# Four layers in one kernel: how the second layer's last image is scaled and the third layer begins, and the order of the last layer's first convolution

## The chip, the cores and the metric

The kernel runs on one core of a Trainium2 chip. The metric is the device time of one execution in microseconds (us); three runs of the kernel before gave 6766.48 (median), 6764.02 and 6773.46. A profiled execution leaves the times of every instruction on the engines: TensorE (PE, with its weight loads PEld), VectorE (DVE), ScalarE (ACT), GpSimd (POOL), and SyncE (SP), which issues all the DMA transfers here.

## The reference

An input of 4 images, 192 channels, 56 x 56 pixels, float32, goes through four layers one after the other. All shapes stay `(4, 192, 56, 56)`.

```python
# layer 0: local attention; batch statistics first
mean = jnp.mean(x, axis=(0, 2, 3)); var = jnp.var(x, axis=(0, 2, 3))
qkv = conv1x1(bn(x), qkv_w, qkv_b)            # 6 heads of 32
attn = softmax(conv7x7(cat(q * scale, k), dm_w) + dm_b + rel_bias, axis=2)   # 49 weights a pixel
out = sum over the 49 neighbours of attn * v
x1 = x + conv1x1(out, proj_w); x = x1 + conv1x1(gelu(conv1x1(x1, c1_w)), c2_w)

# layer 1: a gate for each image and channel
g = relu(bn(conv1x1(x, wg1))).mean((2, 3)) ... filt      # filter from image 0
y = sum(pool7x7(x) * filt); y = relu(bn(y @ w1d[:, :, 1].T + b1d))
x = x * y[:, :, None, None] + x

# layer 2: windows of 8 x 8 at a step of 6, attention in each, folded together;
#          a depthwise 3x3 gate; then gelu, depthwise 3x3, product, projection
# layer 3:
xc, z = split(conv1x1(layer_norm(x), in_proj_w))
xc = silu(depthwise3x3(xc, conv_w) + conv_b)
... four selective scans over xc: rows and columns, forward and backward ...
out = x + conv1x1(layer_norm(y) * silu(z), out_proj_w)
```

The code has three parts: `layers01` for the first two layers, `layer2`, `layer3`. What the code calls the gate (`sc`) is `1 + y` of layer 1.

## The kernel before

**An order written out by a planner.** The instructions of PE, DVE, ACT and POOL are issued in an order that the class `Order` works out when the kernel is built. Every piece of work is a Python generator, a thread, with a place (a number: a smaller one is more urgent). It yields the engine, an assumed duration and the buffers that it needs (`on_pe`, `on_dve`, `on_act`, `on_pool`, `on_sp`), and then issues its instructions. `run` picks again and again the thread with the smallest planned start plus 0.05 us for each unit of its place. It may also yield a condition, such as a mark that another thread sets or the count of a layer's open threads (`order.open`). The assumed durations decide the order alone; on the chip each engine works through its list in that order, and semaphores see to it that data are there and memory is free. The DMA queue of SP is not in the planner's hands: the tile framework orders it.

**Layers 0 and 1** (L370 to L1097). First each image is loaded whole (L402: the first into `x`, the other three into two buffers `xs`), and `bn_stats` goes over it in 14 pieces of 448 pixels (L405). Behind these loads SP issues those of the weights (L406) and of zeros for the padding in `vmem`. The statistics make `bn_c`, which PE needs for its first matmuls (L440). Attention follows: PE makes logits, DVE sums over the neighbours into `oa` and `ob` (L807 to L825), and `mlp` reads these by transposes (L854), and stores each chunk to `mid` in DRAM (L943). When an image is done, `gate(b)` works out `sc` (L1063 to L1066); then, for each of 7 chunks, it loads both halves of the channels from `mid` into an `xc` buffer (L1072), multiplies each half by `sc` (ACT, L1077, for images 0 to 2; POOL, L1080, for image 3) and stores the result (L1082). Those stores are layer 2's input, image by image.

**Layer 2** (L1105 to L1731) starts its preparation when the attention sums are done: weights, small constants, cleared buffers. At L1214 it waits until no thread of layers 0 and 1 is open, then gives their memory back and takes its own. From there: clears of `xns` (DVE, L1228), `qs`, `ks` and `accs` (POOL, L1231, L1234). Then bands of 12 rows go through `front` (loads of `bxl` L1293, edges on POOL L1298 to L1307, layer norm L1249 to L1271, projections L1318), `quad` (attention in four windows: copies on POOL L1607, PE L1617 and L1637, DVE L1650 to L1661, ACT, PE, DVE L1711), `back`, and in chunks of 8 rows through `head`, `grow` (buffer `z1`) and `tail`. The depthwise convolutions of `head` and `tail` are `dwconv` (L1397, L1399): nine taps, and within a tap 2 or 3 independent parts.

**Layer 3** (L1734 to L2244) begins with seven chunks of 8 rows of image 0 in `begin(0, c)`: edges of `pad` on POOL (L1866 to L1872), layer norm (L1825 on DVE, square on ACT, L1838 on PE, two ACT operations, L1844 on DVE), projections L1878 on PE into `pad` by ACT (L1889), then a depthwise 3 x 3 convolution. For image 0 this is done on DVE (L1912 for the first tap, L1914 for eight more, each adding to what the last one left in `u`), for half the channels at a time; after each half the thread yields to PE and ACT for that half of `z` (L1935, L1939). For images 1 to 3 PE does the convolution with diagonal matrices (L1921). `begin(b, c + 1)` may start when chunk c's `pad` is written, and its place is 6 behind that of c. Scans follow (`scan`, L2116 on: DVE L2128, L2144, L2160, POOL L2167, PE L2138, L2183); the first row scans run while later chunks are begun, and the columns (L1975) need all seven.

**Memory.** Tiles come from stacks on the left and on the right of SBUF. `const`, `per` and `p1` of layers 0 and 1 lie on the left, from the bottom up in the order in which they were opened, with `oa` and `ob` in `per`. Layer 2's `xns`, `qs`, `ks`, `accs` are laid out from the bottom of the left after these are closed, in this order. What reuses memory waits for the last reader and writer of the old tiles at that address, stores to DRAM among them.

Of the kernel before, what the change touches and what calls it, by code (L numbers as in the profile page):

```python
# [227 lines left out]
def pixels(ap):  # L228

    return ap.rearrange("(h p) n -> p h n", p=HALF)  # L230
# [122 lines left out]
def on_act(*n, takes=(), table=None, ready=None):  # L353
    return "ACT", sum(0.2 + 0.0009 * i for i in n), takes, table, ready
# [15 lines left out]
def layers01(tc, pools, x_in, packs, aps, dst):  # L370
# [5 lines left out]
    nc = tc.nc  # L376

    ctx, early, dram, banks = pools["01"], pools["01 sums"], pools["dram"], pools["banks"]
    const = ctx.enter_context(tc.tile_pool(name="a_const", bufs=1))
    att = early.enter_context(tc.tile_pool(name="a_att", bufs=1, side="right"))  # L380
    dram = dram.enter_context(tc.tile_pool(name="a_dram", bufs=1, space=DRAM))
# [13 lines left out]
    nc.vector.memset(zero, 0.0)  # L395
    bn_a = const.tile([HALF, 2], F32, name="bn_a")
    bn_c = const.tile([HALF, 2], F32, name="bn_c")
    with tc.tile_pool(name="a_stat", bufs=2) as sp:
        stats = sp.tile([HALF, 2, B * NCHUNK, nc.vector.BN_STATS_DIM], F32, name="stats", bufs=1)
        for b in range(B):  # L400
            t = x[:HALF] if b == 0 else sp.tile([HALF, 2, HW], F32, name="xs")
            nc.sync.dma_start(t, pixels(x_in[b]))  # L402
            for h in range(2):
                for c in range(NCHUNK):
                    nc.vector.bn_stats(stats[:, h, b * NCHUNK + c, :], t[:, h, c * CH : (c + 1) * CH])  # L405
        w = load_packs(nc, const, packs, aps)  # L406
        nc.sync.dma_start(v_bias, aps["vb"].to_broadcast([112, C]))
        for v in vmem:
            for g in range(NG):
                for y in (0, PADW - 3):  # L410
                    nc.sync.dma_start(v[g][:, y : y + 3].rearrange("x y c -> x (y c)"), zero)
                for y in (0, PADW - 3):
                    nc.sync.dma_start(
                        v[g][y : y + 3].rearrange("x y c -> y x c"), zero.rearrange("p (x c) -> p x c", c=64)
                    )
        mv = sp.tile([HALF, 2, 2], F32, name="mv", bufs=1)
        for h in range(2):
            nc.vector.bn_aggr(mv[:, h, :], stats[:, h].rearrange("p a b -> p (a b)"))
        std = sp.tile([HALF, 2], F32, name="std", bufs=1)
        nc.vector.tensor_scalar_add(std, mv[:, :, 1], EPS)  # L420
        nc.scalar.activation(std, std, AF.Sqrt)
        nc.vector.reciprocal(std, std)
        nc.vector.tensor_mul(bn_a, w["a96.bn_gamma"], std)
        nc.vector.tensor_mul(bn_c, mv[:, :, 0], bn_a)
        nc.vector.tensor_sub(bn_c, w["a96.bn_beta"], bn_c)
# [65 lines left out]
    def keep(name, shape, n, rows=128, pool=per):  # L491
        return [pool.tile([rows, *shape], F32, name=f"{name}{i}") for i in range(n)]
# [10 lines left out]
    for t in (*qk_in, *xc, *lg):  # L503
# [11 lines left out]
        rsum=keep_att("rsum", [2, 28], 3, 112),  # L515
        qs=qk_sum,
        lg=lg,
        oa=keep("oa", [28, 128], 2, 112),
        ob=keep("ob", [28, 64], 2, 112),
        hm=keep("hm", [CH], 2),  # L520
    )
    take, done = order.take, order.done
# [509 lines left out]
    def gate(b):  # L1032

        yv = p1.tile([HALF, 2], F32, name="yv")
        for h in range(2):
            yield on_dve(H * DCT, 49, 49)
            r2 = p1.tile([HALF, DCT * DCT], F32, name="pool_y")
            nc.vector.tensor_reduce(
                r2.rearrange("p (a b) -> p a b", b=DCT),
                pool_of[b][:, h].rearrange("p (a i b) -> p a b i", i=H // DCT, b=DCT),  # L1040
                AX.X,
                ALU.add,
            )
            nc.vector.tensor_mul(r2, r2, filt[:, h])
            nc.vector.tensor_reduce(yv[:, h : h + 1], r2, AX.X, ALU.add)
        done(pool_of[b])
        yield on_dve(2)
        nc.vector.tensor_scalar_mul(yv, yv, 1.0 / 64.0)
        yield on_pe(4 * 80, "bank")
        pt = take()  # L1050
        py = pt[:HALF, :2]
        for h in range(2):
            for k in range(2):
                nc.tensor.matmul(
                    py[:, h : h + 1],
                    w["a96.w1T"][:, k, HALF * h : HALF * h + HALF],
                    yv[:, k : k + 1],
                    start=(k == 0),
                    stop=(k == 1),
                )  # L1060
        yield on_dve(2, 2, 2)
        sc = p1.tile([HALF, 2], F32, name="sc")
        nc.vector.tensor_mul(sc, py, s1)  # L1063
        done(pt)
        nc.vector.tensor_add(sc, sc, t1)
        nc.vector.tensor_scalar(sc, sc, 0.0, 1.0, ALU.max, ALU.add)  # L1066
        passed.add(("gate", b))
        for c in range(NCHUNK):
            px = slice(c * CH, (c + 1) * CH)
            yield on_sp("xc")  # L1070
            xt = take("xc")
            nc.sync.dma_start(xt[:HALF], pixels(mid[b])[:, :, px])  # L1072

            for h in range(2):
                if b < B - 1:
                    yield on_act(CH, ready=None if h else order.end + 3)
                    nc.scalar.activation(xt[:HALF, h], xt[:HALF, h], AF.Copy, scale=sc[:, h : h + 1])  # L1077
                else:
                    yield on_pool(CH, each=0.0015)
                    nc.gpsimd.tensor_scalar_mul(xt[:HALF, h], xt[:HALF, h], sc[:, h : h + 1])  # L1080
            yield on_sp()
            nc.sync.dma_start(pixels(dst[b])[:, :, px], xt[:HALF])  # L1082
            done(xt)
# [21 lines left out]
def layer2(tc, order, pools, src, packs, aps, dst):  # L1105
# [28 lines left out]
    (p,) = keep("bp", [2, HW], 1)  # L1134
    (apad,) = keep("bapad", [2, 11, W + 2], 1, HALF)
    zpads = keep("bzpad", [3, 12, W + 2], 2)
    z1 = const.tile([128, 3, 10, W], F32, name="bz1")
    g = const.tile([128, 3, 10, W], F32, name="bg")
    pr = p.rearrange("p h (y x) -> p h y x", x=W)
    ident = const.tile([128, 128], F32, name="b_ident")  # L1140
# [70 lines left out]
    nc.vector.tensor_scalar_mul(w["b96.hft_w"], w["b96.hft_w"], 3.0)  # L1211


    yield lambda: order.open["01"] == 0  # L1214
    pools["01"].close()
    p2 = ctx.enter_context(tc.tile_pool(name="b_2", bufs=1, side="right"))
    left = pools["2 quads"].enter_context(tc.tile_pool(name="b_quads", bufs=1))

    def keep_left(name, shape, n, rows=128):
# [3 lines left out]
    qs = keep_left("bq", [2, BR, PADW], 2, HALF)  # L1223
    ks = keep_left("bk", [2, BR, PADW], 2, HALF)
    accs = keep_left("bacc", [2, 2, BR, PADW], 2)
    for i in range(2):
        yield on_dve(1700)
        nc.vector.memset(xns[i], 0.0)  # L1228
        for t in (qs[i], ks[i]):
            yield on_pool(1600, each=0.0009)  # L1230
            nc.gpsimd.memset(t, 0.0)  # L1231
    for t in accs:
        yield on_pool(3400, each=0.0009)
        nc.gpsimd.memset(t, 0.0)  # L1234
# [46 lines left out]
    def front(j):  # L1281
# [3 lines left out]
        rows = ((3, 6), (9, 5)) if r == 0 else ((2, 9),) if r == NB - 1 else ((2, 6), (8, 6))  # L1285

        yield lambda: at["front"] == j and gone("values", 5 * (j - 1) - 1)
        loads = []
        for i, n in rows:
            y = 12 * r + i - 3  # L1290
# [443 lines left out]
def layer3(tc, order, pools, src, packs, aps, dst):  # L1734
# [80 lines left out]
    def gone(*what):  # L1815
        return what in passed
# [30 lines left out]
    def begin(b, c):  # L1847
# [51 lines left out]
        at = y0 - (8 * c - 1)  # L1899
        px = slice(y0 * W, y1 * W)  # L1900
        zt = None
        for h in range(2):
            pz = pc = uh = None
            if b == 0:

                for t in range(9):
                    yield on_dve(n * W, each=0.0012, ready=order.end - 0.3 if t else None)
                    v = pad[:HALF, h, at + t // 3 : at + t // 3 + n, t % 3 : t % 3 + W]
                    uh = rows2(u[:HALF, h, px])
                    wt = w["c96.conv_w"][:, h, t : t + 1]  # L1910
                    if t == 0:
                        nc.vector.tensor_scalar(uh, v, wt, w["c96.conv_b"][:, h : h + 1], ALU.mult, ALU.add)  # L1912
                    else:
                        nc.vector.scalar_tensor_tensor(uh, v, wt, uh, ALU.mult, ALU.add)  # L1914
            if uh is None:
                yield lambda: gone("diagonals")
            for t in range(9 if uh is None else 0):
                yield on_pe(n * W, *(("bank",) if t == 0 else ()), ready=order.end - 0.5 if t else None)
                if t == 0:
                    pc = take()  # L1920
                nc.tensor.matmul(  # L1921
                    rows2(pc[:HALF, : n * W]),
                    diag[:, h, t],
                    pad[:, h, at + t // 3 : at + t // 3 + n, t % 3 : t % 3 + W],
                    start=(t == 0),
                    stop=(t == 8),
                )
            if uh is None:
                yield on_act(n * W)
                nc.scalar.activation(  # L1930
                    u[:HALF, h, px], pc[:HALF, : n * W], AF.Identity, bias=w["c96.conv_b"][:, h : h + 1]
                )
                done(pc)
            yield on_pe(2 * CH, "bank")
            pz = project(2 + h)  # L1935
            yield on_act(CH, takes=() if h else ("gate",))
            if h == 0:
                zt = take("gate")
            nc.scalar.activation(zt[:, h], pz[:HALF, :CH], AF.Identity, bias=in_b[:, 2 + h : 3 + h])  # L1939
            done(pz)  # L1940
# [342 lines left out]
```

## Time and profile before

| what | us |
|---|---|
| three runs: median (lowest, highest) | 6766.48 (6764.02, 6773.46) |
| the profiled execution: its own time | 6756.62 |
| span from its first to its last instruction | 6754.8 |
| DVE busy, share of the span | 5976.0, 88% |
| PE busy | 5757.1, 85% |
| ACT busy | 2615.2, 39% |
| POOL busy | 1414.7, 21% |
| mean granted clock of TensorE | 0.931 of full |

Stretches of the span, from the view by windows (busy us of each engine):

```profile
2928.00:2960.00 32.00, 2.14 (x4) 0.57 (x2) 0.33 (x3) 0.00 (x0) 19.38 (x14) 0.50 0.41 119
2960.00:2993.00 33.00, 18.25 (x95) 11.03 (x97) 6.04 (x6) 9.80 (x17) 18.34 (x23) 0.73 0.06 16
2993.00:3100.00 107.00, 92.87 (x1516) 60.74 (x1502) 79.77 (x167) 54.23 (x96) 31.44 (x60) 0.97 0.07 19
4857.00:4990.00 133.00, 95.09 (x235) 33.75 (x236) 115.45 (x174) 70.66 (x94) 26.75 (x25) 0.85 0.34 88
```

The columns are the stretch, its length, then busy time and number of instructions of PE, PEld, DVE, ACT and POOL, the granted clock, the DMA engines' share, and GB/s. The first two stretches lie between the last gate of layer 1 and the first full bands of layer 2; the last one holds most of layer 3's first convolution. A busy share says how full an engine was, not that it set the end; for that one reads what ended each wait, which the timeline gives in brackets behind an instruction ("[32.47 <-DMA x<-xc]": the engine had been idle for 32.47 us, until that transfer).

### The profile page before, as it was taken

The page shows a single profiled execution, that of the slowest core. Times are in us where ns is not written, and L with a number is a line of the kernel's source. Part 1 is how long each engine was busy: PE and PEld are TensorE (multiplying, and loading weights), DVE is VectorE, ACT ScalarE, POOL GpSimd, SP SyncE. Part 2 cuts the span into 40 slices and gives each one's busy share as a digit, 9 for nine tenths or more (in the row PEclk, how much of TensorE's full clock was granted, in tenths as well). Part 3 has the DMA queues.
Part 4 walks back from the last instruction along what each step waited for, and adds up shares of the span by engine and source line. Part 5 has one row for each costly group of instructions (what it writes and reads, how often), then busy time and mean ns, then how long its engine had stood idle before and what let it go on. Part 6 is the DMA issues. An engine that isn't in the chain of part 4 may idle for free.

```text
span 6754.8 us, 107251 instructions
## 1 busy us (share of the span) xinstructions
PE 5757.1 (85%) x43558; PEld 2642.5 (39%) x43558; DVE 5976.0 (88%) x7515; ACT 2615.2 (39%) x4049; POOL 1414.7 (21%) x1413
## 2 busy tenths in 40 slices
PE   6999889999999995768888788786689889889776
PEld 3444444444444442335444444453222222222211
DVE  2999999999999999838999899898888887887997
ACT  1121121222222121125555455454366566566544
POOL 0000000000000000132222222221025544545564
PEclk9999889999999997889999899998799999999998
DMA  4222112221222112210000000000045555655654
GB/s 107 59 53 59 36 30 62 52 67 34 54 56 73 30 44 75 62 42 16 18 18 16 18 19 15 18 18 22 23 113 134 150 144 131 161 134 138 171 149 118
DMA packets 252042, 462.65 MB, mean 68 GB/s; under 512 B 30388, under 2 KB 237964, under 8 KB 240412
## 3 DMA queue, kind: packets, MB, share of 16 engines
q1 hardware_dynamic: 251548, 455.80, 26.8%
q8 instruction: 343, 5.62, 0.4%
q14 instruction: 151, 1.24, 0.1%
HBM read 238.58 MB, written 62.96 MB: 45 GB/s over the span
## 4 chain that ended last, share of the span: by engine, by line
DVE 26%; PE 20%; issue 4%; ACT 4%; POOL 1%; DMA 1%; SPq 0%; DVEq 0%; POOLq 0%; ACTq 0%
DVE bg L1399 6%; PE bank L1921 4%; DVE st L2160 3%; DVE bxn L1399 3%; PE bank L1878 2%; DVE bank L2144 2%; PE bank L2138 2%; PE bank L2183 2%; PE bank L1562 1%; PE bank L1265 1%; DVE bacc L1711 1%; PE bank L2011 1%; PE bank L1249 1%; DVE e L1650 1%; PE bank L1488 1%
## 5 line engine op out<-in xcount | busy, mean ns | idle before, releaser
L811 DVE TENSOR_TENSOR pr<-vdx,attn 112x1792 f32<-112x1792 f32 (+4 forms) x720 | 1185.9, 1648 | 19.2
L656 PE MATMUL bank<-qk_in,w_a 64*49 64x392 f32 x9408 | 1157.4, 496 | 0.0
L2167 POOL TENSOR_TENSOR da<-st,bc 128x448 f32<-128x448 f32 x672 | 857.3, 1281 | 844.2 <-DVE st L2160 630.3
L816 DVE TENSOR_TENSOR oa<-oa,pr 112x1792 f32<-112x1792 f32 (+1 forms) x423 | 765.0, 1808 | 0.0
L656 PE MATMUL bank<-qk_in,wd 64*49 64x392 f32 x4032 | 691.3, 494 | 0.0
L2160 DVE TENSOR_TENSOR_SCAN st<-da,st,bank 128x448 f32<-128x448 f32 x576 | 646.8, 1132 | 0.7 <-ACT da L2113 0.7
L656 PEld LDWEIGHTS bank<-qk_in,w_a 64*49 64x49 f32 x9408 | 431.7, 120 | 396.1 <-issue 390.4
L1147 POOL MEMSET bxl<- 128x1008 f32 x3 | 2.7, 938 | 2783.3 <-DVE ob L825 2783.3
L2144 DVE TENSOR_TENSOR bank<-bank,bc 128x448 f32<-128x448 f32 x672 | 382.7, 617 | 114.6 <-PE bank L2138 114.1
L331 ACT ACT_TABLE_LOAD x373 | 478.6, 1283 | 6.7
L2113 ACT ACTIVATE da<-da,a_neg 128x448 f32<-128x448 f32 x672 | 413.8, 658 | 111.7 <-DMA da<-dt 109.6
L1399 DVE SCALAR_TENSOR_TENSOR bg<-bzpad,w_b,bg 128x448 f32<-128x448 f32 (+2 forms) x672 | 423.6, 685 | 0.0
L2183 PE MATMUL bank<-da,w_c 128*32 128x448 f32 x1344 | 355.5, 575 | 72.7 <-POOL da L2167 66.9
L816 DVE TENSOR_TENSOR ob<-ob,pr 112x1792 f32<-112x1792 f32 (+3 forms) x282 | 393.1, 1394 | 0.0
L902 ACT ACTIVATE hm<-bank,w_a 128x448 f32<-128x448 f32 x168 | 106.4, 634 | 637.3 <-PE bank L893 617.8
L2138 PE MATMUL bank<-du,w_c 32*128 32x448 f32 x1344 | 261.6, 626 | 105.0 <-DVE du L2128 62.8
L656 PEld LDWEIGHTS bank<-qk_in,wd 64*49 64x49 f32 x4032 | 247.8, 119 | 256.7 <-issue 254.8
L893 PE MATMUL bank<-xc,w_a 128*128 128x448 f32 x672 | 296.8, 571 | 58.6 <-DVE xc L878 58.6
L608 ACT ACTIVATE qk_in<-bank,qk_bias,qk_scale 64x224 f32<-64x224 f32 (+5 forms) x288 | 146.3, 526 | 445.5 <-PE bank L593 443.2
L1488 PE MATMUL bank<-bxn,w_b 128*128 128x448 f32 (+2 forms) x672 | 291.4, 562 | 22.5 <-DVE bxn L1271 17.1
L908 PE MATMUL bank<-hm,w_a 128*96 128x448 f32 x672 | 288.5, 561 | 20.2 <-ACT hm L902 20.2
L1921 PE MATMUL bank<-pad,diag 128*96 128x448 f32 (+2 forms) x756 | 297.4, 543 | 2.3 <-ACT pad L1889 2.3
(309 smaller groups left out, 9908.4 us busy)
## 6 DMA issues: line engine op xcount, KB each, us to landing
da<-dt SPq DMA_DIRECT2D x672, 224.0 KB
vdx<-vmem SPq DMA_DIRECT2D x168, 476.0 KB
bc<-prod SPq DMA_DIRECT2D x224, 224.0 KB
row<-x SPq DMA_DIRECT2D x56, 336.0 KB
x<-x SPq DMA_DIRECT2D x4, 2352.0 KB
vmem<-vt SPq DMA_DIRECT2D x56, 168.0 KB
xc<-x SPq DMA_DIRECT2D x56, 168.0 KB
mid<-xc SPq DMA_DIRECT2D x56, 168.0 KB
```

The costliest lines, as they stand in the source:

```text
L331: self.nc.scalar.preload_act_table_set(table)
L656: nc.tensor.matmul(py[a][outs[g], : 7 * W].rearrange("p (y x) -> p y x", x=W), wt[halves[a], dx], q[halves[a], r, i0 + m : i0 + m + 7, dx ...
L811: nc.vector.tensor_mul(pr, vv, wt)
L816: nc.vector.tensor_add(og, og, before)
L1399: nc.vector.scalar_tensor_tensor(dst, x, wt[:, t : t + 1], dst, ALU.mult, ALU.add)
L1921: nc.tensor.matmul(rows2(pc[:HALF, : n * W]), diag[:, h, t], pad[:, h, at + t // 3 : at + t // 3 + n, t % 3 : t % 3 + W], start=(t == 0), ...
L2113: nc.scalar.activation(da, da, AF.Exp, scale=a_neg[:, k, g : g + 1])
L2138: nc.tensor.matmul(tiles[j][:, :SCH], w["c96.rep"][r], du[r], start=True, stop=True)
L2144: nc.vector.tensor_mul(tiles[j][:, :SCH], tiles[j][:, :SCH], b_)
L2160: nc.vector.tensor_tensor_scan(sts[j][:, r], da[:, r], tiles[j][:, :SCH][:, r], first, ALU.mult, ALU.add)
L2167: nc.gpsimd.tensor_mul(da, sts[j], c_)
L2183: nc.tensor.matmul(py[32 * j : 32 * j + 32, :SCH], w["c128.sum"], das[j], start=True, stop=True)
```

## The change

- The last image's scaling goes through two new small buffers `xg` (one half of one chunk each, 448 values) and always runs on ACT: 14 loads, 14 operations, 14 stores. `xg` and that image's `sc` live in a pool of their own on the right, which is closed with layer 2's.
- When the last gate is known, a mark is set. Layer 2 takes over the memory of layers 0 and 1 when this mark is there and one of their threads is left open, the one that scales. Its fronts of image 3 wait until that thread is done too.
- `oa` and `ob` get a pool that is opened first on the left; `z1` moves to a pool that is opened later.
- The clears of `xns`, `qs`, `ks` are dealt out anew: the first of each on DVE, the second on POOL.
- The statistics at the start load images 1 to 3 in 21 chunks of 448 pixels through five buffers, and both halves of a chunk follow each other.
- In `begin(0, c)` each tap of the convolution is issued for both halves in turn (planned at 2 x (0.08 + 0.00105 x 448) us in place of 0.08 + 0.0012 x 448 for one half), and both halves' projections of `z` follow after all nine taps.

```diff
+    last = pools["2"].enter_context(tc.tile_pool(name="a_last", bufs=1, side="right"))
+    sc_last = last.tile([HALF, 2], F32, name="sc_last")
+    osum = ctx.enter_context(tc.tile_pool(name="a_osum", bufs=1))
     const = ctx.enter_context(tc.tile_pool(name="a_const", bufs=1))
...
-    with tc.tile_pool(name="a_stat", bufs=2) as sp:
+    with tc.tile_pool(name="a_stat", bufs=5) as sp:
...
+        nc.sync.dma_start(x[:HALF], pixels(x_in[0]))
         for b in range(B):
-            t = x[:HALF] if b == 0 else sp.tile([HALF, 2, HW], F32, name="xs")
-            nc.sync.dma_start(t, pixels(x_in[b]))
-            for h in range(2):
-                for c in range(NCHUNK):
-                    nc.vector.bn_stats(stats[:, h, b * NCHUNK + c, :], t[:, h, c * CH : (c + 1) * CH])
+            for c in range(NCHUNK):
+                px = slice(c * CH, (c + 1) * CH)
+                t = x[:HALF, :, px]
+                if b > 0:
+                    t = sp.tile([HALF, 2, CH], F32, name="xs")
+                    nc.sync.dma_start(t, pixels(x_in[b])[:, :, px])
+                for h in range(2):
+                    nc.vector.bn_stats(stats[:, h, b * NCHUNK + c, :], t[:, h])
...
-        oa=keep("oa", [28, 128], 2, 112),
-        ob=keep("ob", [28, 64], 2, 112),
+        oa=keep("oa", [28, 128], 2, 112, osum),
+        ob=keep("ob", [28, 64], 2, 112, osum),
+        xg=keep("xg", [CH], 2, HALF, last),
...
+        if b == B - 1:
+            order.marks.add("last gate")
+            for c in range(NCHUNK):
+                for h in range(2):
+                    px = slice(c * CH, (c + 1) * CH)
+                    yield on_sp("xg")
+                    xt = take("xg")
+                    nc.sync.dma_start(xt, mid[b][HALF * h : HALF * h + HALF, px])
+                    yield on_act(CH, ready=order.end + 3)
+                    nc.scalar.activation(xt, xt, AF.Copy, scale=sc[:, h : h + 1])
+                    yield on_sp()
+                    nc.sync.dma_start(dst[b][HALF * h : HALF * h + HALF, px], xt)
+                    done(xt)
+            return
...
-    yield lambda: order.open["01"] == 0
+    yield lambda: order.open["01"] == 1 and "last gate" in order.marks
     pools["01"].close()
     p2 = ctx.enter_context(tc.tile_pool(name="b_2", bufs=1, side="right"))
+    z1 = p2.tile([128, 3, 10, W], F32, name="bz1")
...
-    for i in range(2):
-        yield on_dve(1700)
-        nc.vector.memset(xns[i], 0.0)
-        for t in (qs[i], ks[i]):
-            yield on_pool(1600, each=0.0009)
-            nc.gpsimd.memset(t, 0.0)
+    for t in (xns[0], qs[0], ks[0]):
+        yield on_dve(1450)
+        nc.vector.memset(t, 0.0)
+    for t in (xns[1], qs[1], ks[1]):
+        yield on_pool(1600, each=0.0009)
+        nc.gpsimd.memset(t, 0.0)
...
+        yield lambda: b < B - 1 or order.open["01"] == 0
...
-        for h in range(2):
-            pz = pc = uh = None
-            if b == 0:
-
-                for t in range(9):
-                    yield on_dve(n * W, each=0.0012, ready=order.end - 0.3 if t else None)
+        if b == 0:
+
+            for t in range(9):
+                yield on_dve(n * W, n * W, ready=order.end - 0.1 if t else None)
+                for h in range(2):
                     v = pad[:HALF, h, at + t // 3 : at + t // 3 + n, t % 3 : t % 3 + W]
                     uh = rows2(u[:HALF, h, px])
...
+        else:
+            yield lambda: gone("diagonals")
+        for h in range(2):
+            pz = pc = None
+            for t in range(9 if b else 0):
```

More of the change, by code (lines that the diff above doesn't have):

```diff
@@ L1061, in gate @@
         yield on_dve(2, 2, 2)
-        sc = p1.tile([HALF, 2], F32, name="sc")
+        sc = sc_last if b == B - 1 else p1.tile([HALF, 2], F32, name="sc")
         nc.vector.tensor_mul(sc, py, s1)
@@ L1072, in gate @@
             nc.sync.dma_start(xt[:HALF], pixels(mid[b])[:, :, px])
+            yield on_act(CH, CH, ready=order.end + 3)
             for h in range(2):
[L1075 to L1080, printed above, removed]
+                nc.scalar.activation(xt[:HALF, h], xt[:HALF, h], AF.Copy, scale=sc[:, h : h + 1])
             yield on_sp()
@@ L1136, in layer2 @@
     zpads = keep("bzpad", [3, 12, W + 2], 2)
-    z1 = const.tile([128, 3, 10, W], F32, name="bz1")
     g = const.tile([128, 3, 10, W], F32, name="bg")
@@ L1914, in begin @@
                         nc.vector.scalar_tensor_tensor(uh, v, wt, uh, ALU.mult, ALU.add)
-            if uh is None:
-                yield lambda: gone("diagonals")
-            for t in range(9 if uh is None else 0):
+        else:
[3 more added lines that the diff above has]
+            for t in range(9 if b else 0):
                 yield on_pe(n * W, *(("bank",) if t == 0 else ()), ready=order.end - 0.5 if t else None)
@@ L1927, in begin @@
                 )
-            if uh is None:
+            if b:
                 yield on_act(n * W)
```

## The prediction

> **What bounds the kernel now.** I read the page's second part first: the busy share of each engine in 40 slices of 168.9 us.
>
> ```profile
> PE   6999889999999995768888788786689889889776
> DVE  2999999999999999838999899898888887887997
> ```
>
> VectorE is full in nearly every slice but the first and the 17th and 18th (2702 to 3040 us). So time is to be had in the hole at 2900, where layer 2 starts; elsewhere only by taking work from VectorE. The merged timeline of the hole, engine by engine:
>
> ```profile
> 2928.23 0.17 DVE L1066 TENSOR_SCALAR sc<-sc 96x2 f32<-96x2 f32 x1
> 2960.86 1.50 DVE L1228 MEMSET bxn<- 128x1736 f32 x1 [32.47 <-DMA x<-xc]
> ...
> 2928.57 8.30 POOL L1080 TENSOR_SCALAR xc<-xc,sc 96x448 f32<-96x448 f32 x6 [61.51 <-DVE sc L1066]
> 2941.98 8.30 POOL L1080 TENSOR_SCALAR xc<-xc,sc 96x448 f32<-96x448 f32 x6 [5.10 <-DMA xc<-mid]
> 2954.65 2.78 POOL L1080 TENSOR_SCALAR xc<-xc,sc 96x448 f32<-96x448 f32 x2 [4.38 <-DMA xc<-mid]
> 2960.47 1.54 POOL L1231 MEMSET bq<- 96x1736 f32 x1 [3.04 <-issue]
> ...
> 2966.41 5.92 POOL L1234 MEMSET bacc<- 128x3472 f32 x2
> ...
> 2974.03 6.57 PE L1318 MATMUL bank<-bxn,w_b 128*96 128x336 f32 x16 [5.59 <-POOL bxn L1307]
> ```
>
> The gate of the last image is known at 2928.40. GpSimd then scales that image until 2957.43; the last store lands, and only then (2960.86) may VectorE clear `bxn`. The first convolution of layer 2 (L1318) starts at 2974.03, released by GpSimd's L1307, behind its clears. The chain of waits runs there too: POOL `bq`, `bk`, `bacc`, then PE L1318.
>
> The second place is layer 3's first convolution (L1912, L1914), beside layer 2's depthwise convolution (L1399), which has independent parts side by side:
>
> ```profile
> 4721.88 1.87 DVE L1399 SCALAR_TENSOR_TENSOR bg<-bzpad,w_b,bg 128x448 f32<-128x448 f32 x3
> ...
> 4887.48 1.07 DVE L1825 TENSOR_TENSOR row<-row,bank 96x896 f32<-96x896 f32 x1
> 4888.48 0.50 DVE L1912 TENSOR_SCALAR u<-pad,w_c 96x448 f32<-96x448 f32 x1
> 4889.01 5.70 DVE L1914 SCALAR_TENSOR_TENSOR u<-pad,w_c,u 96x448 f32<-96x448 f32 x8
> 4894.63 1.08 DVE L1844 TENSOR_TENSOR row<-row,bank 96x896 f32<-96x896 f32 x1
> 4898.64 0.51 DVE L1912 TENSOR_SCALAR u<-pad,w_c 96x448 f32<-96x448 f32 x1 [2.94 <-ACT pad L1889]
> ```
>
> Eight taps that each read the sum of the one before take 5.70 us: seven steps and one duration of 0.69, so 0.716 us a step. Three independent ones take 1.87: (1.87 - 0.67) / 2 = 0.60 a step.
>
> **The change, part by part.** The sum is made against the profiled execution: span 6754.8, its own time 6756.62, so 1.8 lie around the span. The median of the three runs, 6766.48, is 9.9 above it; I add that at the end.
>
> *1. Layer 2 starts at the gate instead of behind the last store.* The new condition is the mark set right after L1066 and one open thread. `oa` and `ob` now lie first on the left: 2 x 14,336 + 2 x 7,168 = 43,008 bytes per partition. `bxn`, `bq`, `bk` need 6 x 6,944 = 41,664, so they fall on `oa` and `ob` alone, last read at 2888, and wait for no store. From 2928.6 (L1080's start now) GpSimd has three clears (3 x 1.49 = 4.5), `bacc` (5.87) and L1298 to L1307 (2972.33 to 2973.98: 1.65): L1318 can start at 2940.7. VectorE's side: three clears of 1.5 to 2932.9, then from L1251 to the end of L1271 as now (2964.10 to 2970.32: 6.2) to 2939.1. The later one decides: 2974.0 - 2940.7 = **-33.3**. Bounds: if GpSimd clears ahead of the gate, as its empty queue allows from 2888 on, VectorE's side decides, -34.8, and with a PE clock that does not fall to the 0.50 of 2928 to 2960 (L1318 x16 took 6.57 there, 4.08 at 2986) some -37. Below: a clear that still waits for the stores leaves only what the clears' new split saves, one of four 1.49 us clears on GpSimd, -1.5; that case is a rival.
>
> *2. The scaling on ACT.* Removed: 14 GpSimd operations of 1.40 us. Added: 14 on ACT at the 0.66 us of L1077 (same form, images 0 to 2) = 9.2 us, and 28 transfers of 168 KB for 14 of 336 KB: 14 more issues of 0.3 us on SP's queue, which has nothing else due there but the `bxl` loads. They are spread by the order's own reckoning: load, 3 us, scale, store, 2.5 us, about 7.3 us a piece, so some 100 us. ACT is busy 54.2 of 107 us from 2993 to 3100, so most fit into holes, but layer 2's first bands are a chain (VectorE, ACT, PE in turn) and what queues behind a scale on ACT is `bsq`, `bank` and `bq`, for which PE and then VectorE wait. I take a third of 9.2: **+3**. Bounds: 0, and 9.2 plus waits for the load. L1077 waited 24.2 us for `xc<-mid` in 42 pieces, 8.1 for 14: +17.
>
> *3. Statistics by chunks.* Now the four images land at 14.33, 25.0, 35.8 and 46.9, the last 14 statistics take 7.47, and PE starts at 57.23 on `bn_c`. After, two statistics (1.07) follow the last chunk: VectorE is done 6.4 earlier. But the weights are behind the images: DMA still moves 352 and 310 GB/s from 45 to 55 us and 47 after, and PE's first operand is in `w_a`. The same bytes have to land by about 55, so **-2**. Bounds -6.4 (weights not awaited) and +3 (21 issues of 0.44 us put the weights' issue from 33 to about 40 and the transfers run dry in between). The gain would carry: PE is busy 20.00 of 20 us slices from 160 on, VectorE 98%. `z1`'s new place, the clears dealt out anew and `sc_last` cost nothing beside what is in term 1: `z1` is first written tens of us later.
>
> *4. Both halves in turn.* Instructions stay: 126. Of these 112 follow their own half's previous tap; at 0.716 - 0.597 each that is at most -13.4 us, if VectorE alone sets the pace. It doesn't: the halves were a cover. In the rows above the next band's layer norm runs between them: L1825 before half 1, L1844 after it, and the 6.45 us from L1825 to the last `bank` exponential (4887.48 to 4893.93) hide behind 6.2 us of half 1. Then VectorE idles for L1878 and `pad` (2.94, 4.08, 4.52). In the new code all nine pairs come without a yield to PE or ACT, and a band's thread outranks the next band's by 6 places, 0.3 us, so nothing of the next band gets between. A band becomes 18 x 0.597 = 10.7, L1825 to exponential 6.45, L1844 1.1, PE and `pad` 3.5: 21.8 us. The bands now start at 4879.77, 4898.64, 4918.53, 4940.23, 4963.26 and end at 4979.7: 18.9, 19.9, 21.7, 23.0, 16.4. The later ones already hold 7.5 to 8.9 us of scan work, which fits into the new holes (21.8 - 10.7 - 2.1 = 9.0). So +2.8 in front (band 1, where L1825 moves behind half 1), +2.9, +1.9, +0.1, -1.2, and -4.4 in the last band: **+2.1**. Bounds -13.4 and +14 (five bands at +2.8).
>
> For the taps, the Trainium skill, "VectorE: DVE Perf Modes", section "The DRAIN you can't avoid", speaks against the change: each operation is followed by a flush that cannot be skipped by chaining without semaphores. By that rule term 4 would have nothing to gain and would be the lost cover alone. The two step times above differ by 0.12 us, so here the rows decide.
>
> A side effect is bounded too. GpSimd's copies L1607 take 0.4 us, and the longest 21.3, exactly while VectorE runs L1399 without a gap (4207.7 to 4229): taps without gaps hold GpSimd's products of the scan (L2167) back by up to 10.7 us a band. No scan is due yet in most of that stretch; it is inside the +14.
>
> **Sum.** 6756.6 - 33.3 + 3 - 2 + 2.1 = 6726.4; plus 9.9 for the median: **6736**. The greedy order is worked out anew from the start of layer 2 on, for 3,800 us; I allow 10 us either way for its other choices.
>
> **The rivals.**
> - *The halves pay in full.* If the order does find work for the holes, term 4 is -13.4 instead of +2.1: 6736 - 15.5 = 6720. For it: VectorE is busy 19.4 of 20 us from 4920 on. Against: the three waits for `pad` before that.
> - *The start is hidden by something else.* A clear waits for a late reader of old memory, or the chain of L1293, L1251, L1318 is held by its loads. Between -1.5 and -33.3 of term 1 is then left; the middle, -17: 6736 + 16 = 6752, at the worst 6768. For it: the 45 us in which ACT, PE and VectorE all wait at once. Against: the byte count above, and `bxl` loaded at 2850.
> - *Slower: ACT's scales stand in its queue behind loads that SP holds.* SP's queue is in order, and it waits long for `bxl` buffers: L1293 for `bxn` 316 us in 19 times, and three issues took from 2964.92 to 2995.99. An `xg` load behind such a wait comes 15 us late, and ACT, with `bsq` and `bank` behind the scale, stands still. It decides from the third such piece: 3 x 15.5 = 46 against a net gain of 30: 6736 + 46 = 6782. Against: SP's queue took loads early before (L1072 at 2881.74 for a scale at 2928.57).
>
> **How the numbers follow.** Forecast 0.57; halves in full 0.14; hidden start 0.17; slower 0.12. A change of 0.2% (13.5 us) is about what a measurement of this kernel tells from none. The first two lie under 6753; the third straddles it, and I count a third of it (0.05) as under, as the stores are what it would wait for: faster 0.76, within 0.2% 0.12, slower 0.12. The forecast's own range is 6718 to 6752 (ACT up to +17, halves -13 to +14, order 10, not all at once). For 8 in 10 it goes to the lower rival less the order's 10 us and to the hidden start plus 10: 6708 to 6764.
>
> **What would show it.** Term 1: L1228 follows L1066 within a microsecond or two and L1318 starts 10 to 14 us after it, not 46. Term 2: scales of 0.66 us on ACT over some 100 us; ACT's waits for `xg` under 8 us in all. Term 3: PE's first L440 at about 55. Term 4: taps 0.60 apart, L1825 and L1844 no longer between halves, bands about 22 us apart with idle VectorE before L1844 and before the next L1912. If layer 2's last store comes some 30 us earlier but the end does not, term 4 or the new order took it; if L1318 is not earlier, term 1 is wrong and with it the prediction.

## The result and the profile after

The changed kernel takes 6772.68 us (median of 12 runs, 6759.68 to 6782.72). The kernel before, run beside it on the same chip, takes 6762.44 (12 runs, 6754.06 to 6773.46). The ratio is 1.0019, with a 95% interval of 1.0011 to 1.0026: about 13 us slower, a small change, but the interval leaves out 1. 6736 was predicted, with 6718 to 6752 as the range: the 30 us that were to be won are missing.

The profiled execution of after took 6759.68 us, the fastest of its twelve, with a span of 6757.9 (before: 6756.62 and 6754.8). The second part of its page, in the same 40 slices as before:

```profile
PE   6999889999999995878888788876679889899777
DVE  2999999999999999848899899988777888887997
```

Beside before's row, VectorE's 18th slice (2872 to 3041 us, the start of layer 2) has gone from 3 to 4. Against that the 20th (3210 to 3379) has gone from 9 to 8, and the 29th to 31st (4730 to 5237, the first bands of layer 3) from 8 to 7. So VectorE is fuller at the start and emptier later. The merged timeline at the last gate (start, length, engine, line, and in brackets how long the engine had been idle and what released it):

```profile
2920.88 0.17 DVE L1075 TENSOR_SCALAR sc_last<-sc_last 96x2 f32<-96x2 f32 x1
2921.08 1.23 ACT L1086 ACTIVATE xg<-xg,sc_last 96x448 f32<-96x448 f32 x2 [8.16 <-DVE sc_last L1075]
2921.65 1.50 DVE L1246 MEMSET bxn<- 128x1736 f32 x1 [0.60 <-issue]
...
2926.04 0.67 ACT L1086 ACTIVATE xg<-xg,sc_last 96x448 f32<-96x448 f32 x1 [3.73 <-DMA xg<-mid]
2926.70 0.79 DVE L1269 TENSOR_TENSOR bxn<-bxl,bank 96x672 f32<-96x672 f32 x1
...
2931.92 0.67 ACT L1086 ACTIVATE xg<-xg,sc_last 96x448 f32<-96x448 f32 x1 [4.10 <-DMA xg<-mid]
...
2933.95 0.76 ACT L1278 ACTIVATE bsq<-bxn 96x672 f32<-96x672 f32 x1
...
2937.04 0.67 ACT L1086 ACTIVATE xg<-xg,sc_last 96x448 f32<-96x448 f32 x1 [2.34 <-DMA xg<-mid]
2937.73 1.28 ACT L331 ACT_TABLE_LOAD   x1
...
2939.02 0.51 ACT L1286 ACTIVATE bank<-bank,b_eps 96x336 f32<-96x336 f32 x1
...
2940.02 0.85 DVE L1289 TENSOR_TENSOR bxn<-bxn,bank 96x672 f32<-96x672 f32 x1 [12.53 <-ACT bank L1287]
...
2940.97 7.80 PE L1337 MATMUL bank<-bxn,w_b 128*96 128x336 f32 x16 [3.66 <-issue]
```

(L1075, L1269, L1278, L1337 of after are L1066, L1251, L1260, L1318 of before.) VectorE clears `bxn` 0.6 us behind the gate, as the change wants. Then it waits 12.53 us for ACT: `bsq`, due at 2927.5, starts at 2933.95, because four scales that wait for their loads stand ahead of it, and the two operations of the layer norm stand behind another. PE's first convolution comes 20.1 us after the gate. It came 45.8 us after it before.

How much of these 25.7 us is left later is seen best when every execution is counted from its own gate (L1066), since the gate itself falls between 2920.9 and 2940.3 us in the profiles of this study (see the end). From the traces of before, of after and of the first of the experiments below:

| us after the gate | before | after | after, halves as before (e1) |
|---|---|---|---|
| first convolution of layer 2 (L1318) | 45.8 | 20.1 | 20.2 |
| last store of layer 2 (L1580) | 1940.3 | 1943.3 | 1943.2 |
| 97th scan of 672 (L2160) | 2299.9 | 2319.5 | 2303.2 |
| end | 3826.5 | 3837.0 | 3819.3 |

Layer 2 started 25.7 us earlier and ended 3.0 us later: 28.7 us are lost inside it. Between its end and the 97th scan after loses another 17 on before, and e1, which differs only by the convolution's halves, next to nothing. VectorE's idle time since the gate, summed from the trace, says when the first loss happens (the last row is for an experiment told below, with before's order behind the early start):

```
us after the gate     50    200    350    450    800   1200   1600   1900
before              45.3   88.6  103.4  107.1  125.7  161.6  192.6  233.4
after               35.4   65.7   82.7  101.7  120.7  153.7  193.1  232.1
e5                  35.8   63.6   78.8   82.6  102.2  136.5  168.7  206.6
```

After's lead is 23 us at 200, 21 at 350, and 5.4 at 450; at 1600 nothing is left. Behind the 97th scan after and e1 make up 9 and 11 us on before; before's profile has a granted clock of 0.84 from 5360 to 5420 us (after 0.91), which may be why, but no run here shows it. VectorE's timeline of after in the worst stretch, 405 to 430 us behind the gate:

```profile
3329.36 0.96 DVE L1680 TENSOR_TENSOR e<-e,mx 128x768 f32<-128x768 f32 x1
3332.24 0.68 DVE L1589 SCALAR_TENSOR_TENSOR bp<-bank,w_b,bp 96x448 f32<-96x448 f32 x1 [1.91 <-PE bank L1581]
3336.36 0.68 DVE L1589 SCALAR_TENSOR_TENSOR bp<-bank,w_b,bp 96x448 f32<-96x448 f32 x1 [3.44 <-PE bank L1581]
3341.87 0.85 DVE L1289 TENSOR_TENSOR bxn<-bxn,bank 96x672 f32<-96x672 f32 x1 [4.83 <-ACT bank L1287]
3349.26 1.55 DVE L1269 TENSOR_TENSOR bzpad<-bzpad,bank 128x1344 f32<-128x1344 f32 x1 [6.55 <-PE bank L1267]
```

Bands of images 0 and 1 run side by side here: GpSimd's edges of image 1's first band come 280 us after the gate. Each operation but the first waits for PE or ACT, and nothing else stands between them in VectorE's order.

### The profile page after: what moved, and what is told of

It is laid out like the page before. It is cut to its first block, busy times and chain, and to the rows that moved or that the text cites. A ratio compares the mean times of both kernels' runs of the same rounds, so it can differ in the third digit from the quotient of the medians.

```text
span 6757.9 us, 107347 instructions
## 1 busy us (share of the span) xinstructions
PE 5740.8 (85%) x43558; PEld 2642.2 (39%) x43558; DVE 5965.2 (88%) x7516; ACT 2628.6 (39%) x4068; POOL 1411.1 (21%) x1398
## 4 chain that ended last, share of the span: by engine, by line
DVE 47%; PE 38%; issue 7%; ACT 5%; DMA 2%; POOL 1%; SPq 0%; DVEq 0%; POOLq 0%; ACTq 0%
DVE pr L820 8%; PE bank L665 7%; DVE oa L825 6%; DVE bg L1418 5%; PE bank L1941 4%; DVE ob L825 4%; DVE bxn L1418 3%; DVE st L2180 3%; PE bank L1897 2%; PE bank L917 2%; PE bank L902 2%; DVE bank L2164 2%; PE bank L2158 2%; PE bank L2203 2%; PE bank L686 1%
## 5 line engine op out<-in xcount | busy, mean ns | idle before, releaser
L665 PE MATMUL bank<-qk_in,w_a 64*49 64x392 f32 x9408 | 1152.3, 494 | 0.0
L665 PE MATMUL bank<-qk_in,wd 64*49 64x392 f32 x4032 | 687.9, 492 | 0.0
L665 PEld LDWEIGHTS bank<-qk_in,w_a 64*49 64x49 f32 x9408 | 430.7, 119 | 391.9 <-issue 387.2
L665 PEld LDWEIGHTS bank<-qk_in,wd 64*49 64x49 f32 x4032 | 247.5, 119 | 257.1 <-issue 255.2
L917 PE MATMUL bank<-hm,w_a 128*96 128x448 f32 x672 | 288.1, 560 | 19.9 <-ACT hm L911 19.9
L686 PE MATMUL bank<-qk_sum,w_a 64*49 64x168 f32 (+1 forms) x5376 | 277.2, 337 | 27.8 <-DVE qk_sum L656 25.8
```

Of the source, the lines that this page charges most:

```text
L665: nc.tensor.matmul(py[a][outs[g], : 7 * W].rearrange("p (y x) -> p y x", x=W), wt[halves[a], dx], q[halves[a], r, i0 + m : i0 + m + 7, dx ...
L917: nc.tensor.matmul(acc[h][:HALF, :CH], w["a128.c2T"][:, m, HALF * h : HALF * h + HALF], hm, start=(m == 0), stop=(m == 5),)
```

## The experiments

Numbers in us; each ratio is to runs of the kernel before made in the same batch.

**e1: the changed kernel with the halves as before.**

```diff
-            for t in range(9):
-                yield on_dve(n * W, n * W, ready=order.end - 0.1 if t else None)
-                for h in range(2):
+        for h in range(2):
+            if b == 0:
+                for t in range(9):
+                    yield on_dve(n * W, each=0.0012, ready=order.end - 0.3 if t else None)
```

> The changed kernel with layer 3's first convolution as before (half after half); all else stays. Theory H: the halves in turn take the cover of the next band's layer norm, and the trace of after shows the lead of 7.5 us at 4880 us turned into a lag of 12.7 us at 5150. Then without it the lead is still there at 5150, some 20 us better than after at that place; at the end 8 to 20 us of it are left: 6753 to 6765. Rival: the halves cost nothing (term 4 of the prediction, +2), and the lead was lost in layer 2 alone: 6768 to 6776.

Measured: 6759.97, ratio 0.9997 (0.9987 to 1.0008). Theory H's time holds; the halves cost 0.0022 of 6760, about 15 us. But without them the kernel is only as fast as before: the start's gain is missing all the same. The "lead of 7.5 us at 4880" of the expectation was the gate's own, 7.4 us earlier in that profile; counted from the gate, layer 3's first tap comes at 1860.4 us in after and 1861.1 in before, so the lead was gone by then.

**e2: the kernel before with only the halves in turn** (the same lines, the other way round).

> The kernel before with nothing but the halves in turn. Theory H: bands of layer 3 about 22 us apart or more, VectorE idle before L1844's successor and the next first tap, 8 to 20 us slower than before: 6770 to 6782. By term 4 as predicted: +2, that is 6762 to 6767. If the halves pay in full: 6749.

Measured: 6775.97, 1.0026 (1.0016 to 1.0036), 16 to 18 us slower. Two bands of layer 3 in e2's timeline of VectorE (L1911 and L1913 are before's L1912 and L1914):

```profile
4887.41 1.09 DVE L1911 TENSOR_SCALAR u<-pad,w_c 96x448 f32<-96x448 f32 x2 [4.42 <-ACT pad L1889]
4888.42 9.61 DVE L1913 SCALAR_TENSOR_TENSOR u<-pad,w_c,u 96x448 f32<-96x448 f32 x16
4897.96 1.07 DVE L1825 TENSOR_TENSOR row<-row,bank 96x896 f32<-96x896 f32 x1
4904.59 1.08 DVE L1844 TENSOR_TENSOR row<-row,bank 96x896 f32<-96x896 f32 x1 [5.56 <-ACT bank L1842]
4910.72 1.09 DVE L1911 TENSOR_SCALAR u<-pad,w_c 96x448 f32<-96x448 f32 x2 [5.05 <-ACT pad L1889]
4911.74 9.61 DVE L1913 SCALAR_TENSOR_TENSOR u<-pad,w_c,u 96x448 f32<-96x448 f32 x16
```

The 16 taps take 9.61 us, 0.596 a step: the step is as short as predicted. L1825 now stands behind all of them, so 5.56 us of idleness follow before L1844 and 5.05 before the next first tap. The band starts of e2 are 27.7, 23.3, 21.9, 25.4 and 22.6 us apart, where before had 22.3, 18.9, 19.9, 21.7 and 23.0. The last tap comes 17 us later after the gate.

**e3 and e4: e1 with the scales planned at another distance behind their loads.** The instructions are those of e1; the list scheduler places them differently.

```diff
-                    yield on_act(CH, ready=order.end + 3)
+                    yield on_act(CH, ready=order.end + 4)      # e3; e4: + 2.5
```

> As e1_old_halves, and each of the 14 scales planned 4 us after its load instead of 3; the same instructions, only the list scheduler's order differs. Theory O: the 30 us won at the gate are lost in layer 2 because the scheduler makes another order of layer 2, whose quality is a matter of small differences; on its own clock this order ends layer 2 26 us earlier than that of e1. So 15 to 26 us faster than e1_old_halves, about 6735 to 6745. Rival C: the lead is lost on the chip whatever the order (VectorE and PE wait for each other at each image's end): within 5 us of e1.

> As e1_old_halves, and each scale planned 2.5 us after its load instead of 3. Theory O: on the scheduler's own clock layer 2 ends 20 us later than in e1, so 10 to 20 us slower than e1_old_halves, about 6768 to 6780. Rival C: within 5 us of e1.

Measured: e3 6729.60, 0.9955 (0.994 to 0.997), 30 us faster than e1; e4 6749.47, 0.998 (0.9971 to 0.9989), 10 faster than e1 where 10 to 20 slower was expected. So the order matters by tens of us, and the scheduler's own clock had e4's sign wrong. The trace of e4 tells why it is a case of its own. ACT's timeline:

```profile
2959.51 0.67 ACT L1086 ACTIVATE xg<-xg,sc_last 96x448 f32<-96x448 f32 x1 [0.46 <-DMA xg<-mid]
2963.36 0.67 ACT L1086 ACTIVATE xg<-xg,sc_last 96x448 f32<-96x448 f32 x1 [3.18 <-DMA xg<-mid]
2964.49 0.67 ACT L1086 ACTIVATE xg<-xg,sc_last 96x448 f32<-96x448 f32 x1 [0.46 <-DMA xg<-mid]
2965.06 0.76 ACT L1278 ACTIVATE bsq<-bxn 96x672 f32<-96x672 f32 x1
```

All 14 scales stand ahead of `bsq`, a pair every 5 us as the two buffers come round, and L1337 starts 38.3 us after the gate. From there VectorE's order is that of before, instruction for instruction (all 5356 from the first L1251 on). So e4 is "before's order, started 7.5 us earlier". In after, e1 and e3 the orders part from before's at the eighth of these instructions.

**e5: the scales take no time in the scheduler's reckoning.**

```diff
-                    yield on_sp("xg")
+                    yield "free", 0.5, ("xg",), None, None
...
-                    yield on_act(CH, ready=order.end + 3)
+                    yield "free", 0.6, (), None, order.end + 3
...
-                    yield on_sp()
+                    yield "free", 0.5, (), None, None
```

> As e1_old_halves (changed kernel, halves as before), but the 14 scales and their transfers take no engine time in the list scheduler's reckoning: it then orders layers 2 and 3 exactly as it does in the kernel before, some 54 us earlier on its own clock, and the scales are dropped in between. Theory O (the lead was lost to the new order of layer 2): the order of before keeps it, layer 2 ends some 25 to 33 us closer to the gate than in before (before: 1940 us after the gate), and the time is 6728 to 6740. Rival C (the chip takes the lead back whatever the order): within 8 us of e1, 6752 to 6768.

Measured: 6731.77, 0.9953 (0.9941 to 0.9965). VectorE's order is before's in all 5356 instructions, and the start is e1's: L1318's counterpart 20.0 us after the gate. The scales lie where e1 has them, the first 0.2 us after the gate in both and the last at 44.2 in e1 and 43.7 in e5, so it isn't their waits on ACT that set the two apart. The last store of layer 2 follows at 1911.8 (before 1940.3, e1 1943.2) and the end at 3798.4 (3826.5). The lead of 25.8 us is kept to the end, where it is 28. Between 350 and 450 us after the gate VectorE is idle for 3.8 us, in after for 19.0 (table above). At the place where after stalls, VectorE's timeline of e5 reads:

```profile
3326.25 0.93 DVE L1678 TENSOR_REDUCE mx<-e 128x12 f32<-128x768 f32 x1
3327.11 1.06 DVE L1669 TENSOR_TENSOR e<-bank,w_b 128x256 f32<-128x256 f32 x3
3328.11 0.94 DVE L1680 TENSOR_TENSOR e<-e,mx 128x768 f32<-128x768 f32 x1
3328.97 0.93 DVE L1678 TENSOR_REDUCE mx<-e 128x12 f32<-128x768 f32 x1
3329.84 0.66 DVE L1589 SCALAR_TENSOR_TENSOR bp<-bank,w_b,bp 96x448 f32<-96x448 f32 x1
3330.43 0.94 DVE L1680 TENSOR_TENSOR e<-e,mx 128x768 f32<-128x768 f32 x1
3331.29 0.78 DVE L1383 TENSOR_TENSOR bacc<-bacc 96x616 f32<-96x616 f32 x1
3332.00 1.53 DVE L1269 TENSOR_TENSOR bzpad<-bzpad,bank 128x1344 f32<-128x1344 f32 x1
3333.47 0.67 DVE L1589 SCALAR_TENSOR_TENSOR bp<-bank,w_b,bp 96x448 f32<-96x448 f32 x1
```

Between the two L1589, which in after wait for PE, stand L1680, L1383 and L1269. After has done its L1680 ahead of the first L1589, and comes to its L1269 on `bzpad` at 3349.26, behind both. This is one way in which an order loses time without an instruction more.

**e6: before with the halves in turn, and room between the pairs of taps.**

```diff
-                yield on_dve(n * W, n * W, ready=order.end - 0.1 if t else None)
+                yield on_dve(n * W, n * W, ready=order.end + 0.5 if t else None)
```

> The kernel before with the halves in turn, but each pair of taps is reckoned ready 0.5 us after the pair before it instead of 0.1 us before its end, so that the next band's layer norm gets in between the pairs (L1825 behind the fourth pair, L1844 behind the last). Theory H (the loss of e2, 16 us, is the lost cover): bands of 16 to 19 us, and 0 to 10 us faster than before: 6750 to 6762. Rival (the halves in turn cost by themselves, or scans pushed back cost): 6768 to 6778, as e2.

Measured: 6759.17, 0.9997 (0.9987 to 1.0006). A band of e6 in VectorE's timeline:

```profile
4905.47 3.65 DVE L1913 SCALAR_TENSOR_TENSOR u<-pad,w_c,u 96x448 f32<-96x448 f32 x6
4909.04 1.07 DVE L1825 TENSOR_TENSOR row<-row,bank 96x896 f32<-96x896 f32 x1
4910.04 6.04 DVE L1913 SCALAR_TENSOR_TENSOR u<-pad,w_c,u 96x448 f32<-96x448 f32 x10
4915.99 1.08 DVE L1844 TENSOR_TENSOR row<-row,bank 96x896 f32<-96x896 f32 x1
4923.28 0.51 DVE L1911 TENSOR_SCALAR u<-pad,w_c 96x448 f32<-96x448 f32 x1 [6.21 <-ACT pad L1889]
```

L1844 follows the last tap without a wait, and e2's loss is gone: it was the lost cover. The wait for `pad` before the next band stays (6.21). The bands are 23.4, 18.7, 19.3, 17.7 and 18.9 us apart (16 to 19 were expected). The last tap comes 8.5 us earlier after the gate than in before (2043.0 against 2051.5), but the end only 0.4: the row scans, which before did between the bands, wait until later. Even with cover, nothing is won at the end.

**e7: before with only the statistics by chunks** (the lines of the diff at the `a_stat` pool).

> The kernel before with nothing but the statistics by chunks. Predicted term 3: 2 us faster (bounds 6.4 faster, 3 slower), and the gain carried to the end: 6755 to 6761. Rival: PE's first work comes earlier but nothing is left at the gate, 6759 to 6762.

Measured: 6757.83, 0.9997 (0.9988 to 1.0006): 2 us faster by the ratio, with an interval from 8 faster to 4 slower. PE's first work (L440) starts at 55.37, against 57.23 in before; in the other profiles it lies between 53.2 and 56.4 with the chunks, and between 56.3 and 57.7 without them. The time agrees with the prediction and can't be told from nothing.

**e8: before with another order and the same work.**

```diff
-                    best.append((t + self.HURRY * th[0], th[1], t, th))
+                    best.append((t + (0.048 if th[5] == "2" else self.HURRY) * th[0], th[1], t, th))
```

> The kernel before, the same work and the same start of layer 2; only the weight with which the list scheduler prefers older work is 0.048 instead of 0.05 for layer 2's threads, which gives another order. Theory O: order alone moves layer 2's end by 10 to 30 us either way (its own clock says 30 us earlier at layer 2's end and 7 us at the end): the time leaves before's by 8 us or more. Rival C: within 5 us of before.

Measured: 6760.88, 1.0002 (0.9992 to 1.0012). Here theory O's expectation fails: this order, which parts from before's after 833 of VectorE's instructions, ends layer 2 9.7 us earlier after the gate, has the 97th scan 10.5 later, and the end 0.4 later. Another order need not cost or bring anything.

**e9 and e10: the changed kernel whole, with the scales unplanned as in e5;** e10 with e6's room between the pairs as well.

> The changed kernel whole, halves in turn included, with the scales taking no time in the list scheduler's reckoning (as e5). If the two losses are separate and add up (31 us by the new order of layer 2, 13 to 16 us by the halves), it is 13 to 16 us slower than e5_scales_unplanned: 6745 to 6748. If they are one (the halves only cost where the order is bad): 6730 to 6738.

> As e9, and the taps' pairs spaced in the reckoning as in e6, so that the next band's layer norm gets in between. By e6 the cover is back and nothing is won beyond it: 6728 to 6735, equal to e5 within 4 us. If the halves in turn pay once they have their cover (0.12 us for 112 steps, 13.4 us): 6718 to 6725.

Measured: e9 6739.84, 0.9972 (0.996 to 0.9983); e10 6737.05, 0.9965 (0.9951 to 0.9978). With e1, e5 and after, e9 makes a square of ratios:

| layer 2's order | halves as before | halves in turn |
|---|---|---|
| as in before | e5 0.9953 | e9 0.9972 |
| as the change makes it | e1 0.9997 | after 1.0019 |

By rows the halves cost 13 and 15 us, by columns the order 30 and 32: as far as these ratios tell, the two losses are separate and add up. The intervals are some 8 us wide to either side, and those of e5 and e9 just overlap. By the medians e9 is 8 us behind e5, and its 6739.84 lies between the two expectations; by the ratios it is 13, at the lower edge of the first. e10 isn't faster than e5, so the halves in turn don't pay with cover either; whether it is slower by a few us can't be told.

**e11 and e12: e1 with the scales planned 3.5 and 6 us behind their loads** (as e3).

> As e1_old_halves, each scale planned 3.5 us after its load. Another new order of layer 2. Theory S (the scheduler's own clock ranks the orders that start at the same place: e1 ended layer 2 at 5221.0 on it and 1943 us after the gate on the chip, e3 at 5194.7 and 1909): here 5227.6, so 1943 to 1955 us and 6758 to 6772. Rival (the clock tells nothing, orders are a lottery): anywhere from 6728 to 6760.

> As e1_old_halves, each scale planned 6 us after its load. Theory S: 5206.4 on the scheduler's clock, between e3 and e1, so 1920 to 1930 us after the gate and 6738 to 6750. Rival: anywhere from 6728 to 6775.

Measured: e11 6738.32, 0.9967 (0.9954 to 0.9979); e12 6722.28, 0.9949 (0.9936 to 0.9962). Theory S falls with e11: the order that ends last on the scheduler's clock is 20 us faster than e1's. e12 has the lowest time of the study, 34 us under before; e3 and e5 lie within its interval. In its merged timeline three scales stand ahead of `bsq`, where after has six:

```profile
2934.38 0.79 DVE L1269 TENSOR_TENSOR bxn<-bxl,bank 96x672 f32<-96x672 f32 x1
...
2935.33 0.78 ACT L1278 ACTIVATE bsq<-bxn 96x672 f32<-96x672 f32 x1 [0.87 <-DVE bxn L1269]
...
2940.80 4.54 PE L1337 MATMUL bank<-bxn,w_b 128*96 128x336 f32 x10 [2.08 <-POOL bxn L1326]
```

`bsq` follows L1269 at once, and the convolution starts 12.2 us after the gate, held by GpSimd's clears. All orders beside each other, from their traces (layer 2 is from its first convolution to its last store):

| kernel | start after gate | length of layer 2 | ratio |
|---|---|---|---|
| before | 45.8 | 1894.5 | 1 |
| e4, e5 (before's order) | 38.3, 20.0 | 1891.0, 1891.8 | 0.998, 0.9953 |
| e8 | 45.8 | 1884.9 | 1.0002 |
| e3 | 15.0 | 1893.5 | 0.9955 |
| e12 | 12.2 | 1900.1 | 0.9949 |
| e11 | 20.2 | 1905.3 | 0.9967 |
| e1, after | 20.2, 20.1 | 1923.0, 1923.2 | 0.9997, 1.0019 |

## Why the prediction was wrong

**The step that failed** is the allowance for the greedy order: "I allow 10 us either way for its other choices". The orders tried here make layer 2 between 1884.9 and 1923.2 us long, and the one that the change draws is the longest, 28.7 us above before's. That is more than the 25.7 that the start won. With before's order and everything else of the change (e9) the kernel gains 19 us (0.9972) of the 30 predicted. That its 6739.84 is near 6736 is in part luck: the before of e9's batch is at 6760.48, and the sum started from 6766.48. What is short there is in terms 1 and 4, below. Put together for after, from the gate on: 25.7 won at the start, 28.7 lost in layer 2, 13 to 18 lost at the halves.

**Term 1, the start (-33.3): right in mechanism, too large.** No store is waited for, and the clears follow the gate within a microsecond. L1318 comes 20.1 us after the gate, not 10 to 14, so -25.7. The missing 7.6 us are ACT's. With the scales planned later (e12) the start is at 12.2, and GpSimd's clears decide, as the working had it.

**Term 2, the scaling on ACT (+3): its place was wrong.** It costs nothing that shows once layer 2 runs (e5's layer 2 takes 1891.8 us with the scales in it, before's 1894.5 in the same order), but it stands ahead of `bsq` in the very chain that term 1 shortens: against e12's 12.2 us that is 7.9 us in after and 26.1 in e4. The waits for `xg` are 12.4 us in 6 times, and under 8 was given as the mark. The slower rival named this queue; its price of 46 us was never reached, because the loads did not wait for `bxl` in SP's queue; they came as the two `xg` buffers did, a pair every 5 us.

**Term 3, statistics by chunks (-2): agrees, but can't be told from nothing.** PE's first work is at 54.49 in after (about 55 was the mark), and e7 gives -2, within 6 either way.

**Term 4, both halves in turn (+2.1): the mechanism was right, the size wrong.** It measured 13 to 18 us by the ratios (e9 against e5, e1 against after, e2), about the upper bound of 14 or above it. The working had the band at 21.8 us throughout; after has 26.0, 23.0, 21.7, 25.3 and 22.5. It also let the later bands' scan work fill the new holes; in e2 the row scans begin 23 us later instead (2030.2 us after the gate against 2007.1).

The prediction weighed a rule of the Trainium skill here ("VectorE: DVE Perf Modes", section "The DRAIN you can't avoid"). The rule says that the flush behind each operation can't be skipped by chaining without semaphores. The same section adds that a next operation which isn't held back starts earlier, and the prediction left that out. The runs show 0.596 us a step in turn against 0.716 in a dependent chain, so taking the rows was right. But the 13 us of shorter steps never reach the end, not even with cover (e6, e10).

**The rivals.** The halves did not pay in full. The start was not hidden. "Slower", at 0.12, was nearest to the outcome, by another mechanism.

**What stays open:** why one order of layer 2 is 30 us longer than another. The stall between 350 and 450 us shows one way in which time is lost, and it isn't the whole: there e3 and e12, which are fast, idle for 14.1 and 11.8 us themselves, after for 19.0, before for 3.8 and e5 for 3.8. No run here tells beforehand which order is good; the scheduler's own clock does not.

## What to carry to other kernels

Where a scheduler works out the whole order anew, an early start is worth only what the new order leaves of it. Make the added work invisible to the scheduler, or try several placements of it, before the change itself is judged. In an engine's queue that runs in order, put an operation that waits for a transfer behind the next link of the critical chain, not ahead of it. Interleaving two dependent chains shortens the steps, but takes away the second chain as cover for everything that waits for the first.

## What the runs showed of the hardware

The same instructions did not reach the same place at the same time. Up to the last gate, after and e3 issue the same work; the gate came at 2920.9 in the one and at 2940.2 in the other, and between 2920.9 and 2940.3 over all profiles, those of kernels that start otherwise among them. The windows' view of PE (stretch, length, busy us and instructions, granted clock, DMA share, GB/s), first after, then e3:

```profile
60.00:260.00 200.00, 196.63 (x2087) 1.00 0.21 50
260.00:460.00 200.00, 198.11 (x2236) 0.98 0.22 52
```

```profile
60.00:260.00 200.00, 196.97 (x2048) 0.98 0.20 48
260.00:460.00 200.00, 198.07 (x2184) 0.96 0.23 53
```

PE is full in both, and the granted clock differs by 0.02, some 8 us in these 400; the matmul of L665 that begins at 453.7 in after begins at 461.6 in e3. The rest of the 19 us at the gate is not traced here. This is why single profiles were compared from the gate on. It also fits that e3's profiled execution (6744.89), with its late gate, is the slowest of its six runs.
